# Attention in groups of three key blocks with three score slots, and a depthwise convolution taken wholly by TensorE

## The chip, the cores and the metric

The kernel runs on one core of a Trainium2 chip. The metric is device time in microseconds (us) of one launch. Before the change it is 4289.91 us, the median of three runs (4288.64 to 4290.33). Lines like `L223` are lines of the kernel before the change unless "after" is said; in the changed kernel the same statements stand some lines further on (the score product is L223 in both, the projections move from L397 and L409 to L405 and L417, the depthwise convolution from L873 to L880).

## The reference

Four residual layers over `x` of shape (4, 256, 48, 48), so B = 4 images, 256 channels, N = 2304 positions, all float32:

```python
x = x + L0(_gn(x))   # 8 heads of 64: q, k l2-normed over the head's 64 channels, softmax(10 q.k), v, w_out
x = x + L1(_gn(x))   # max pool, blur pool, four depthwise convolutions, sigmoid gate
x = x + L2(_gn(x))   # one head of 64: softmax(theta.phi / 8), g, W_w, batch norm over the images
x = x + L3(_gn(x))   # squeeze gate, depthwise 3x3, instance norm, leaky relu
```

```python
# layer 0
q = _l2norm_last(q)
k = _l2norm_last(k)
sim = jnp.einsum('bhdi,bhdj->bhij', q, k) * SCALE
attn = jax.nn.softmax(sim, axis=-1)
out = jnp.einsum('bhij,bhdj->bhid', attn, v)
...
# layer 3
y = xw * a[:, :, None, None]
y = jax.lax.conv_general_dilated(y, refine_w, window_strides=(1, 1), padding='SAME', feature_group_count=C, dimension_numbers=('NCHW', 'OIHW', 'NCHW'))
y = y + refine_b[None, :, None, None]
mu = jnp.mean(y, axis=(2, 3), keepdims=True)
var = jnp.mean(jnp.square(y - mu), axis=(2, 3), keepdims=True)
y = (y - mu) * jax.lax.rsqrt(var + EPS)
return jax.nn.leaky_relu(y, SLOPE)
```

## The kernel before

**Units, groups, steps.** The attention of layers 0 and 2 is one long stream of 108 units. A unit is one image, one pair of heads (layer 0) or two halves of the queries (layer 2), and 384 query columns. There are 16 phases of six units in layer 0 (image b, pair p) and four phases of three units in layer 2. The keys come in 18 blocks of 128 (`JB`). `scores(u, j)` (L223) multiplies one block of keys by the queries, once for each half of the partitions, into a PSUM tile `sc` of two banks, and ScalarE takes the exponential into an SBUF tile `pt` (L229). `weigh(u, j)` (L242) multiplies `pt` by the values and accumulates in the PSUM bank `av` over all 18 blocks. A float32 matmul appears as two PE records.

`attend` goes through the stream in steps of one group of `G = 2` blocks. In step t it issues, in this order: the scores of group t; the sums of the group before (`add_up`); what is due (`finish`); some ticks of the side work; `total`, where one is due; and `weigh` for the group before. The four engines PE, DVE, ACT and POOL keep exactly this written order (`manual_schedule`) until the attention ends. Each engine works through its own queue in order.

**The sums.** `add_up` sums the exponentials for the softmax. In groups 1, 3, 5 and 7 POOL adds the two tiles into `half` (one buffer, L259) and DVE adds `half` to `acc` in the next step (L255); in the other groups DVE adds the tiles itself (L252, L262). A unit takes 13 additions on DVE and 4 on POOL. `total` multiplies `acc` by ones into a bank `pj` (L267), and DVE takes the reciprocal `rinv` (L272, in `total`). `divide`, one step later, reads the sum on ScalarE for a check (L279), multiplies `av` by `rinv` on DVE (L282) and checks `rinv` on ScalarE (L284). Two steps follow in which one `out_proj` product each is made (L441) and added to x by DVE (L446, L450).

**The side work** comes as generators in lanes, merged tick by tick and spread over the steps of a phase. `project` makes q, k and v of the next pair: for each of six chunks, `normed` (DVE, L374), q and k products (L397), each copied out by DVE (L401) and squared by ScalarE in place (L402), and the v product (L409), copied by ScalarE (L414). In phases p = 1 and p = 2 of images 1 to 3, and in the first two phases of layer 2, a second lane runs layer 1 of the image before: pooling and 80 taps on DVE (L564). `project2` (L617, L628, L641) and `w_stats` (L663, read by `bn_stats` L675) belong to layer 2. Before the stream starts, `project` runs once alone for the first pair.

**PSUM.** Eight banks: two `sc` tiles of two banks, two `av` banks, two `pj` banks. Every product other than scores and values goes through `pj`: `total`, the projections, `out_proj`, `w_stats`, the small products of the group norms.

**Layer 3** is ordered by the framework's scheduler. For each image `before_conv` makes 12 products of W (L663), each scaled by ScalarE (L818) and added to x by POOL (L822), then a group norm and the gate (PE L174, L184, L831, L843, with DVE, POOL and ScalarE between), and at last the padded image on ScalarE (L854). `conv` makes five of the nine taps as matmuls with diagonal matrices (L873, 10 matmuls for each of three steps), ScalarE evacuates (L880), DVE adds the other four taps (L888), takes statistics (L893), ScalarE normalises (L902), DVE applies the leaky relu (L903), POOL adds to x (L904), and a DMA writes the result. The generator `before_conv(b + 1)` fills the steps of `conv(b, .)`.

```python
G = 2
NG = JB // G
PAIRED = (1, 3, 5, 7)
...
    ps_sc = ctx.enter_context(tc.tile_pool(name="ps_sc", bufs=2, space=bass.MemoryType.PSUM))
    ps_av = ctx.enter_context(tc.tile_pool(name="ps_av", bufs=2, space=bass.MemoryType.PSUM))
    ps_pj = ctx.enter_context(tc.tile_pool(name="ps_pj", bufs=2, space=bass.MemoryType.PSUM))
```

Of the kernel before, what the change touches and what calls it, by code (L numbers as in the profile page):

```python
# [9 lines left out]
F32 = mybir.dt.float32  # L10
AF = mybir.ActivationFunctionType
ALU = mybir.AluOpType
AX = mybir.AxisListType

P = 128
HW = 48
# [39 lines left out]
def _drain(gen):  # L56
    for _ in gen:
        pass
# [4 lines left out]

G = 2
NG = JB // G
PAIRED = (1, 3, 5, 7)
NCH = NSL
# [6 lines left out]
def usual_path(  # L74
# [7 lines left out]
    small = ctx.enter_context(tc.tile_pool(name="small", bufs=2))  # L82
    ps_sc = ctx.enter_context(tc.tile_pool(name="ps_sc", bufs=2, space=bass.MemoryType.PSUM))
    ps_av = ctx.enter_context(tc.tile_pool(name="ps_av", bufs=2, space=bass.MemoryType.PSUM))
    ps_pj = ctx.enter_context(tc.tile_pool(name="ps_pj", bufs=2, space=bass.MemoryType.PSUM))

# [121 lines left out]
    big = keep.enter_context(tc.tile_pool(name="big", bufs=2))  # L208
    wqp = main.enter_context(tc.tile_pool(name="wq", bufs=2))
    xsp = main.enter_context(tc.tile_pool(name="xs", bufs=3))  # L210
    op = main.enter_context(tc.tile_pool(name="o", bufs=2))
    ppool = main.enter_context(tc.tile_pool(name="pt", bufs=5))
    apool = main.enter_context(tc.tile_pool(name="acc", bufs=2))
# [33 lines left out]
    def add_up(u, g):  # L247

        pts = [u["pt"][j] for j in range(g * G, (g + 1) * G)]
        if g == 0:  # L250
            u["acc"] = apool.tile([P, 2, SL], F32, tag="acc", name="acc")
            nc.vector.tensor_add(u["acc"], pts[0], pts[1])  # L252
            return
        if u.get("half") is not None:
            nc.vector.tensor_add(u["acc"], u["acc"], u["half"])  # L255
            u["half"] = None
        if g in PAIRED:
            u["half"] = hpool.tile([P, 2, SL], F32, tag="half", name="half")
            nc.gpsimd.tensor_add(u["half"], pts[0], pts[1])  # L259
        else:  # L260
            for pt in pts:
                nc.vector.tensor_add(u["acc"], u["acc"], pt)  # L262

    def total(u):
        u["l"] = pj_tile()
        for h in range(2):
            nc.tensor.matmul(  # L267
                u["l"][h * D : (h + 1) * D, :SL], lhsT=ones, rhs=u["acc"][:, h, :],
                start=True, stop=True,
            )  # L270
        u["rinv"] = rpool.tile([P, SL], F32, tag="rinv", name="rinv")
        nc.vector.reciprocal(u["rinv"], u["l"][:, :SL])  # L272

    finished = {}

    def divide(u):
        i = u["i"]
        junk = rpool.tile([P, SL], F32, tag="junk", name="junk")
        nc.scalar.activation(  # L279
            junk, u["l"][:, :SL], AF.Identity, accum_out=checks[:, 0, i : i + 1]  # L280
        )
        nc.vector.tensor_mul(u["o"](), u["av"][:, :SL], u["rinv"])  # L282
        finished[u["b"]] = finished.get(u["b"], 0) + 1
        nc.scalar.activation(  # L284
            junk, u["rinv"], AF.Identity, accum_out=checks[:, 1, i : i + 1]
        )
# [18 lines left out]
    def attend(phases):  # L305
# [7 lines left out]
        def finish(t):  # L313
            for fn in due.pop(t, ()):
                fn()

        for t, (u, g, st) in enumerate(groups):
            for j in range(g * G, (g + 1) * G):
                scores(u, j)
            if prev is not None:  # L320
                add_up(*prev)
            finish(t)
            if st["gen"] is None:
# [4 lines left out]
            until = -(-st["total"] * st["at"] // (st["n"] - 3))  # L328
            while st["done"] < until and next(st["gen"], st) is not st:
                st["done"] += 1  # L330
            if st["at"] == st["n"] - 1:
                _drain(st["gen"])
            if t in sums:
                total(sums.pop(t))
            if prev is not None:
                pu, pg = prev
                for j in range(pg * G, (pg + 1) * G):
                    weigh(pu, j)
                if pg == NG - 1:
                    sums[t + 1] = pu  # L340
                    due.setdefault(t + 2, []).append(lambda pu=pu: divide(pu))
                    for i, fn in enumerate(pu["after"]):
                        due.setdefault(t + 3 + i, []).append(fn)
            prev = (u, g)
        pu, pg = prev
        add_up(pu, pg)
        for j in range(pg * G, (pg + 1) * G):
            weigh(pu, j)
        for t in sorted(due):
            finish(t)  # L350
# [9 lines left out]
    def project(b, norm, pair):  # L360
# [18 lines left out]
        fetch(0)  # L379
        fetch(1)  # L380
        q = big.tile([P, N], F32, tag="q", name="q")
# [6 lines left out]
        for s in range(NCH):  # L388
            cols = slice(s * SL, (s + 1) * SL)
            if s + 1 < NCH:  # L390
                normed(s + 1)
            if s + 2 < NCH:
                fetch(s + 2)
            for t, to in ((0, q), (1, kk)):
# [12 lines left out]
            for i in range(SL // P):  # L407
# [7 lines left out]
                v[:, j0 : j0 + SL // P, :].rearrange("p j d -> p (j d)"), ps[:, :SL]  # L415
            )
            yield  # L417
        n2 = small.tile([P, 2], F32, tag="n2", name="n2")
# [371 lines left out]


    PE_TAPS = (0, 1, 2, 3, 5)
    DVE_TAPS = (4, 6, 7, 8)
    diag = lp.tile([P, NK, len(PE_TAPS), P], F32, name="diag")
    for k in range(NK):
        for i, t in enumerate(PE_TAPS):
            nc.gpsimd.tensor_scalar(diag[:, k, i, :], ident, rfw[:, k, t : t + 1], None, ALU.mult)
    W2 = HW + 2
# [64 lines left out]
    def conv(b, k):  # L863
# [3 lines left out]
        for c in range(NSL // 2):  # L867
            ps = sc_tile()
            for h in range(2):
                r0 = (2 * c + h) * RS  # L870
                for t in PE_TAPS:
                    dr, dc = divmod(t, 3)
                    nc.tensor.matmul(  # L873
                        ps[:, h, :SL].rearrange("p (r c) -> p r c", c=HW),
                        lhsT=diag[:, k, PE_TAPS.index(t), :],
                        rhs=pad[:, r0 + dr : r0 + dr + RS, dc : dc + HW],
                        start=t == PE_TAPS[0], stop=t == PE_TAPS[-1],
                    )
# [3 lines left out]
                bias=vec[:, V_RB, k : k + 1],  # L882
            )
            yield
        zr = z.rearrange("p (r c) -> p r c", c=HW)
        for t in DVE_TAPS:
            dr, dc = divmod(t, 3)
            nc.vector.scalar_tensor_tensor(  # L888
                zr, pad[:, dr : dr + HW, dc : dc + HW], rfw[:, k, t : t + 1], zr,
                ALU.mult, ALU.add,  # L890
            )
        for s in range(NSL):
            nc.vector.bn_stats(st[:, s, :], z[:, s * SL : (s + 1) * SL])  # L893
        mv = small.tile([P, 2], F32, tag="in_mv", name="in_mv")
# [4 lines left out]
        rsqrt(ri, ve)  # L899
        mr = small.tile([P, 1], F32, tag="in_mr", name="in_mr")  # L900
        nc.vector.scalar_tensor_tensor(mr, mv[:, 0:1], -1.0, ri, ALU.mult, ALU.mult)
        nc.scalar.activation(z, z, AF.Identity, bias=mr, scale=ri)  # L902
        nc.vector.scalar_tensor_tensor(z, z, SLOPE, z, ALU.mult, ALU.max)  # L903
# [857 lines left out]
```

## Time and profile before

The profiled execution took 4289.91 us, of which its span (first to last instruction) is 4287.8 us; 2.1 us lie around it. Its time equals the median of the three runs. The mean granted TensorE clock was 0.963.

| stretch of the trace (us) | what runs | PE busy | DVE busy | PE clock |
|---|---|---|---|---|
| 20.5 to 52.5 (32.0) | the first `project`, alone | 27.95 | 12.80 | 1.00 |
| 249.9 to 449.4 (199.5) | layer 0, image 0, pair 1 | 198.64 | 115.17 | 1.00 |
| 1047.9 to 1274.7 (226.8) | layer 0, image 1, pair 1, with layer 1 beside it | 210.19 | 202.14 | 0.96 |
| 3424.4 to 3581.1 (156.7) | layer 2, image 0, with layer 1 beside it | 123.39 | 136.61 | 0.88 |
| 3865.3 to 3952.7 (87.4) | layer 2, image 3 | 87.40 | 51.35 | 1.00 |
| 3952.7 to 4288.0 (335.3) | the last `w_stats`, then layer 3 | 240.13 | 196.08 | 0.79 |

Of the 16 phases of layer 0 ten last 196.4 to 199.6 us, and the six with layer 1 beside them 226.1 to 234.9 us. Busy times are sums of what the records cover; overlapping matmuls count once. A busy PE is not a PE at its peak, since the ends of matmuls are modelled.

### The profile page before, as it was taken

The page shows a single profiled execution, that of the slowest core. Times are in us where ns is not written, and L with a number is a line of the kernel's source. Part 1 is how long each engine was busy: PE and PEld are TensorE (multiplying, and loading weights), DVE is VectorE, ACT ScalarE, POOL GpSimd, SP SyncE. Part 2 cuts the span into 40 slices and gives each one's busy share as a digit, 9 for nine tenths or more (in the row PEclk, how much of TensorE's full clock was granted, in tenths as well). Part 3 has the DMA queues.
Part 4 walks back from the last instruction along what each step waited for, and adds up shares of the span by engine and source line. Part 5 has one row for each costly group of instructions (what it writes and reads, how often), then busy time and mean ns, then how long its engine had stood idle before and what let it go on. Part 6 is the DMA issues. An engine that isn't in the chain of part 4 may idle for free.

```text
span 4287.8 us, 50150 instructions
## 1 busy us (share of the span) xinstructions
PE 3954.9 (92%) x19538; PEld 1733.6 (40%) x19538; DVE 3034.9 (71%) x3751; ACT 1875.7 (44%) x3062; POOL 1088.3 (25%) x624
## 2 busy tenths in 40 slices
PE   7999999999998899999888999998889977899784
PEld 3444444444433344444333444443334433344442
DVE  4555556556998965569989655699895589955556
ACT  3444444444544444445444445454444433234331
POOL 1222222222222322222223222223232222212352
PEclk9999999999999999999999999999999988899787
DMA  4000000000000000000000000000000000000001
GB/s 148 16 16 19 8 19 8 19 12 15 12 15 12 15 8 19 12 16 12 15 12 15 6 21 12 15 12 12 12 1 1 1 1 1 1 1 1 11 33 45
DMA packets 44326, 67.45 MB, mean 16 GB/s; under 512 B 4336, under 2 KB 42032, under 8 KB 42032
## 3 DMA queue, kind: packets, MB, share of 16 engines
q1 hardware_dynamic: 41216, 62.92, 4.7%
q8 instruction: 155, 2.54, 0.2%
q10 hardware_dynamic: 2864, 1.24, 0.1%
q14 instruction: 91, 0.75, 0.1%
HBM read 54.71 MB, written 9.44 MB: 15 GB/s over the span
## 4 chain that ended last, share of the span: by engine, by line
PE 64%; DVE 29%; issue 3%; ACT 2%; POOL 2%; DMA 0%; DVEq 0%; ACTq 0%; POOLq 0%
PE sc L223 24%; PE av L242 23%; DVE acc L262 8%; DVE l1acc L564 7%; PE pj L397 5%; PE pj L441 3%; PE pj L409 2%; DVE acc L255 2%; PE sc L873 2%; DVE rinv L272 2%; DVE z L888 2%; PE pj L267 1%; PE pj L663 1%; ACT pt L229 1%; DVE xs L374 1%
## 5 line engine op out<-in xcount | busy, mean ns | idle before, releaser
L229 ACT ACTIVATE pt<-sc 128x768 f32<-128x768 f32 x1944 | 1473.6, 808 | 1520.0 <-PE sc L223 1425.3
L259 POOL TENSOR_TENSOR half<-pt 128x768 f32<-128x768 f32 x432 | 853.8, 1976 | 2626.5 <-ACT pt L229 2313.1
L223 PE MATMUL sc<-q,k 64*128 64x384 f32 x6912 | 1363.8, 513 | 52.0 <-ACT pt L229 49.1
L242 PE MATMUL av<-pt,v 128*64 128x384 f32 x6912 | 1321.0, 502 | 0.0
L262 DVE TENSOR_TENSOR acc<-acc,pt 128x768 f32<-128x768 f32 x864 | 946.1, 1095 | 128.1 <-ACT pt L229 42.3
L223 PEld LDWEIGHTS sc<-q,k 64*128 64x128 f32 x6912 | 595.9, 187 | 809.6 <-ACT pt L229 305.1
L242 PEld LDWEIGHTS av<-pt,v 128*64 128x64 f32 x6912 | 433.2, 137 | 725.7 <-issue 713.9
L255 DVE TENSOR_TENSOR acc<-acc,half 128x768 f32<-128x768 f32 x432 | 416.5, 964 | 191.9 <-POOL half L259 191.2
L564 DVE SCALAR_TENSOR_TENSOR l1acc<-pd,grid,l1acc 128x256 f32<-128x256 f32 x640 | 347.3, 543 | 18.2
L272 DVE RECIPROCAL rinv<-pj 128x384 f32<-128x384 f32 x108 | 275.9, 2555 | 109.7 <-PE pj L267 109.6
L397 PE MATMUL pj<-xs,w 128*128 128x384 f32 x768 | 303.0, 520 | 40.2 <-issue 32.7
L402 ACT ACTIVATE pj<-pj 128x384 f32<-128x384 f32 x192 | 91.2, 475 | 403.8 <-DVE q L401 266.3
L441 PE MATMUL pj<-o,wo 128*128 128x384 f32 x384 | 175.7, 539 | 39.2 <-DVE x L450 16.5
L397 PEld LDWEIGHTS pj<-xs,w 128*128 128x128 f32 x768 | 136.3, 194 | 186.0 <-issue 101.5
L450 DVE TENSOR_TENSOR x<-pj,x 128x384 f32<-128x384 f32 x144 | 79.9, 555 | 169.9 <-PE pj L441 169.9
L223 PE MATMUL sc<-qv,kd 64*128 64x384 f32 x864 | 176.5, 527 | 19.1 <-ACT pt L229 19.1
L242 PE MATMUL av<-pt,qv 128*64 128x384 f32 x864 | 192.1, 534 | 0.0
L873 PE MATMUL sc<-pad,diag 128*128 128x384 f32 x480 | 169.1, 510 | 5.7 <-ACT pad L854 5.7
L409 PE MATMUL pj<-w,xs 128*128 128x128 f32 x1152 | 152.8, 283 | 13.7 <-DVE x L450 12.2
L409 PEld LDWEIGHTS pj<-w,xs 128*128 128x128 f32 x1152 | 139.2, 193 | 60.1 <-issue 28.9
L252 DVE TENSOR_TENSOR acc<-pt 128x768 f32<-128x768 f32 x108 | 107.1, 992 | 45.2 <-ACT pt L229 44.8
L166 DVE BATCH_NORM_STATS2 gn_st<-x 128x6 f32<-128x384 f32 x192 | 98.1, 549 | 57.4 <-POOL x L822 57.4
(139 smaller groups left out, 2229.2 us busy)
## 6 DMA issues: line engine op xcount, KB each, us to landing
xs<-in_x_dram SPq DMA_DIRECT2D x96, 384.0 KB, 3.2
x<-in_x_dram SPq DMA_DIRECT2D x8, 1152.0 KB, 8.4
out_dram<-x SPq DMA_DIRECT2D x8, 1152.0 KB, 4.2
w<-in_wqkv_dram SPq DMA_DIRECT2D x32, 192.0 KB, 3.7
wo<-in_wout_dram ACTq DMA_DIRECT2D x1, 512.0 KB, 4.1
dw<-in_dww_dram ACTq DMA_DIRECT2D x1, 132.0 KB, 5.4
wph<-in_thphi_w_dram ACTq DMA_DIRECT2D x2, 64.0 KB, 4.5
Ww<-in_W_w_dram ACTq DMA_DIRECT2D x2, 64.0 KB, 5.0
```

Of the source, the lines that this page charges most:

```text
L223: nc.tensor.matmul(ps[:, h, :SL], lhsT=u["of"]["k"][r, j * P : (j + 1) * P], rhs=u["of"]["q"][r, u["qc"]], start=True, stop=True,)
L229: nc.scalar.activation(pt, ps[:, :, :SL], AF.Exp)
L242: nc.tensor.matmul(u["av"][r, :SL], lhsT=value(u, j, h), rhs=pt[:, h, :], start=j == 0, stop=j == JB - 1,)
L255: nc.vector.tensor_add(u["acc"], u["acc"], u["half"])
L259: nc.gpsimd.tensor_add(u["half"], pts[0], pts[1])
L262: nc.vector.tensor_add(u["acc"], u["acc"], pt)
L272: nc.vector.reciprocal(u["rinv"], u["l"][:, :SL])
L397: nc.tensor.matmul(ps[:, :SL], lhsT=w[:, k, t, :], rhs=xs[s][:, k, :], start=k == 0, stop=k == NK - 1,)
L409: nc.tensor.matmul(ps[:, i * P : (i + 1) * P], lhsT=xs[s][:, k, i * P : (i + 1) * P], rhs=w[:, k, 2, :], start=k == 0, stop=k == NK - 1,)
L441: nc.tensor.matmul(ps[:, :SL], lhsT=wo[:, p, k * P : (k + 1) * P], rhs=o, start=True, stop=True)
L564: nc.vector.scalar_tensor_tensor(acc, src, w, acc, ALU.mult, ALU.add)
L873: nc.tensor.matmul(ps[:, h, :SL].rearrange("p (r c) -> p r c", c=HW), lhsT=diag[:, k, PE_TAPS.index(t), :], rhs=pad[:, r0 + dr : r0 + dr + ...
```

## The change

The attention now goes in groups of three blocks (`G = 3`, six groups to a unit). There are three `sc` tiles (six banks), one `av` bank and one `pj` bank. ScalarE copies the finished `av` into SBUF (`take`, called after the last `weigh` of a unit), and `divide` multiplies that copy. `total` now also reads the sum on ScalarE for the check. In `add_up` POOL adds the first two tiles of groups 1 to 4, and DVE the third; a unit still takes 13 additions on DVE and 4 on POOL. In a step, either the due work is done or one tick, ahead of `total` and `weigh`; further ticks come after `weigh`. The buffers of `pt` go from five to seven, of `xs` from three to two, of `w` from two to one. `normed` of the next chunk moves from the start of a chunk to its end.

In layer 3 all nine taps are matmuls (18 for each of three steps); the four taps on DVE go; statistics are taken after each step, and the normalisation moves from ScalarE (L902) to DVE.

```diff
-G = 2
+G = 3
-PAIRED = (1, 3, 5, 7)
+PAIRED = (1, 2, 3, 4)
...
-    ps_sc = ctx.enter_context(tc.tile_pool(name="ps_sc", bufs=2, space=bass.MemoryType.PSUM))
-    ps_av = ctx.enter_context(tc.tile_pool(name="ps_av", bufs=2, space=bass.MemoryType.PSUM))
-    ps_pj = ctx.enter_context(tc.tile_pool(name="ps_pj", bufs=2, space=bass.MemoryType.PSUM))
+    ps_sc = ctx.enter_context(tc.tile_pool(name="ps_sc", bufs=3, space=bass.MemoryType.PSUM))
+    ps_av = ctx.enter_context(tc.tile_pool(name="ps_av", bufs=1, space=bass.MemoryType.PSUM))
+    ps_pj = ctx.enter_context(tc.tile_pool(name="ps_pj", bufs=1, space=bass.MemoryType.PSUM))
...
-    wqp = main.enter_context(tc.tile_pool(name="wq", bufs=2))
-    xsp = main.enter_context(tc.tile_pool(name="xs", bufs=3))
+    wqp = main.enter_context(tc.tile_pool(name="wq", bufs=1))
+    xsp = main.enter_context(tc.tile_pool(name="xs", bufs=2))
-    ppool = main.enter_context(tc.tile_pool(name="pt", bufs=5))
+    ppool = main.enter_context(tc.tile_pool(name="pt", bufs=7))
...
         pts = [u["pt"][j] for j in range(g * G, (g + 1) * G)]
+        half = u.pop("half", None)
+        if g in PAIRED:
+            u["half"] = hpool.tile([P, 2, SL], F32, tag="half", name="half")
+            nc.gpsimd.tensor_add(u["half"], pts[0], pts[1])
+            pts = pts[2:]
         if g == 0:
             u["acc"] = apool.tile([P, 2, SL], F32, tag="acc", name="acc")
             nc.vector.tensor_add(u["acc"], pts[0], pts[1])
-            return
...
+            pts = pts[2:]
+        if half is not None:
+            nc.vector.tensor_add(u["acc"], u["acc"], half)
+        for pt in pts:
+            nc.vector.tensor_add(u["acc"], u["acc"], pt)
...
+    def take(u):
+        u["araw"] = rpool.tile([P, SL], F32, tag="araw", name="araw")
+        nc.scalar.copy(u["araw"], u["av"][:, :SL])
...
-        nc.vector.tensor_mul(u["o"](), u["av"][:, :SL], u["rinv"])
+        nc.vector.tensor_mul(u["o"](), u["araw"], u["rinv"])
...
-            finish(t)
...
-            while st["done"] < until and next(st["gen"], st) is not st:
+            if t in due:
+                finish(t)
+            elif st["done"] < until and next(st["gen"], st) is not st:
                 st["done"] += 1
-            if st["at"] == st["n"] - 1:
-                _drain(st["gen"])
...
                 if pg == NG - 1:
+                    take(pu)
                     sums[t + 1] = pu
...
+            while st["done"] < until and next(st["gen"], st) is not st:
+                st["done"] += 1
+            if st["at"] == st["n"] - 1:
+                _drain(st["gen"])
...
             if s + 1 < NCH:
-                normed(s + 1)
-            if s + 2 < NCH:
-                fetch(s + 2)
+                fetch(s + 1)
...
+            if s + 1 < NCH:
+                normed(s + 1)
             yield
...
-    PE_TAPS = (0, 1, 2, 3, 5)
-    DVE_TAPS = (4, 6, 7, 8)
-    diag = lp.tile([P, NK, len(PE_TAPS), P], F32, name="diag")
+    diag = lp.tile([P, NK, 9, P], F32, name="diag")
...
-                for t in PE_TAPS:
+                for t in range(9):
...
-        for t in DVE_TAPS:
-            dr, dc = divmod(t, 3)
-            nc.vector.scalar_tensor_tensor(
-                zr, pad[:, dr : dr + HW, dc : dc + HW], rfw[:, k, t : t + 1], zr,
-                ALU.mult, ALU.add,
-            )
...
-        nc.scalar.activation(z, z, AF.Identity, bias=mr, scale=ri)
+        nc.vector.tensor_scalar(z, z, mv[:, 0:1], ri, ALU.subtract, ALU.mult)
```

## The prediction

> **What bounds the kernel now.** I read the page first, for where the bound changes; then the stages, by windows cut where a phase's first exponential starts; then the order of time inside one stage of each kind.
>
> ```profile
> span 4287.8 us, 50150 instructions
> ...
> PE   7999999999998899999888999998889977899784
> ...
> DVE  4555556556998965569989655699895589955556
> ...
> PEclk9999999999999999999999999999999988899787
> ...
> PE 64%; DVE 29%; issue 3%; ACT 2%; POOL 2%; DMA 0%; DVEq 0%; ACTq 0%; POOLq 0%
> ...
> L262 DVE TENSOR_TENSOR acc<-acc,pt 128x768 f32<-128x768 f32 x864 | 946.1, 1095 | 128.1 <-ACT pt L229 42.3
> ```
>
> ```profile
> 249.90:449.40 199.50, 198.64 (x1034) 85.58 (x1032) 115.17 (x131) 98.00 (x163) 44.56 (x25) 1.00 0.05 15
> 1047.90:1274.70 226.80, 210.19 (x1046) 88.64 (x1044) 202.14 (x256) 102.64 (x177) 61.69 (x33) 0.96 0.05 13
> 3952.70:4288.00 335.30, 240.13 (x666) 128.04 (x662) 196.08 (x240) 91.49 (x97) 133.81 (x91) 0.79 0.07 29
> ```
>
> The windows give span, then PE, PEld, DVE, ACT, POOL busy, and the clock. There are three regimes. Ten layer-0 phases are bound by PE (198.64 of 199.5). The six with layer 1 beside them are bound by DVE, closely followed by PE. Layer 3 is bound by neither: its chain passes from PE to DVE and back. So a gain on PE counts only in the first kind, and work moved to PE in layer 3 shows in full once PE fills it.
>
> In order of time, a PE-bound stretch, the end of the attention, and layer 3:
>
> ```profile
> 292.56 1.51 PE L242 MATMUL av<-pt,v 128*64 128x384 f32 x8
> 294.00 1.56 PE L223 MATMUL sc<-q,k 64*128 64x384 f32 x8
> 295.50 0.91 PE L441 MATMUL pj<-o,wo 128*128 128x384 f32 x2
> ...
> 3951.64 2.80 PE L242 MATMUL av<-pt,qv 128*64 128x384 f32 x16
> ...
> 3958.89 13.67 PE L663 MATMUL pj<-y,Ww 64*128 64x384 f32 x22 [2.44 <-ACT junk L279]
> ...
> 4011.72 6.72 PE L873 MATMUL sc<-pad,diag 128*128 128x384 f32 x20
> ...
> 4018.37 1.55 PE L663 MATMUL pj<-y,Ww 64*128 64x384 f32 x4
> ```
>
> Start to start, a value group takes 1.44 us and a score group 1.49; two value groups in a row end 1.29 later than one. So the passage between the two kinds costs 0.15 or more. The convolution takes 6.65 us for 20 records, 0.665 a matmul. And the projections' evacuation:
>
> ```profile
> 296.25 1.45 PE L397 MATMUL pj<-xs,w 128*128 128x384 f32 x4
> ...
> 297.74 0.56 DVE L401 COPY k<-pj 128x384 f32<-128x384 f32 x1 [0.73 <-PE pj L397]
> ...
> 298.33 0.47 ACT L402 ACTIVATE pj<-pj 128x384 f32<-128x384 f32 x1 [1.84 <-DVE k L401]
> 298.71 0.19 ACT L402 ACTIVATION_READ_ACCUMULATOR pj<-pj 128x1 f32 x1
> ```
>
> PE issues its next product at 297.63; the bank is free only at 298.90.
>
> **What the Trainium skill says.** "TensorEngine Tiling (Array Packing)", Key Properties: changing the tiling mode, not just the tile, drains TensorE. The trace agrees: pairs of score matmuls inside a group follow at 0.32, while the first and last of a group take 0.42 to 0.43. "PSUM — Partial Sum Buffer", PSUM bank collisions: two engines on one bank and quadrant must be kept apart by semaphores, so one bank for all products means one product at a time until the last reader is done. The trace agrees: PE waits 2.44 us for the check L279 above. "SBUF — State Buffer", two separate sides: a DVE instruction with two SBUF inputs and a GpSimd one exclude each other for a whole instruction. Here L262 takes 959 ns in the PE-bound phase and 1353 where POOL gets in between. "TensorE: Matmul & The Clock Gate", Part 1: an idle PE falls to half clock. Here one W product takes 1.28 us at the end of the attention and 0.74 between convolutions.
>
> **The change part by part.** The sum is made against the profiled execution's 4289.9 us (span 4287.8 and 2.1 around it), which is the median as well.
>
> *Groups of three, where PE binds.* A pair of matmuls adds 0.32 to a group, so three blocks take (1.49 + 0.64) + (1.44 + 0.64) = 4.21 us, against 1.5 x 2.93 = 4.395: 0.185 less, six times a unit, 1.11 a unit. In the 60 units of the ten phases: -66.6.
>
> *One bank, where PE binds.* In the built order of the changed kernel `total` (L267) comes straight after a q or k product twice, and after a v product once, in each of six phases (pairs 0 to 2 of image 0, pair 0 of the others); once each in pair 3 of images 0 to 2; four `project2` products in the last. After q or k PE stalls 298.96 - 297.63 = 1.33; after v 0.65 (ScalarE copy 0.48 and hand-overs), and the same after a `project2` product. That is 6 x 3.3 + 3 x 2.0 + 2.6 = +28. Elsewhere at least 2.1 us of scores or values lie between two products and cover the 1.33; if DVE is late there, the cover is gone. Sum of both: -38.
>
> *Work hidden here.* `take` (0.48 on ScalarE, 44% busy) ends under the next scores before `av` is needed. The third score slot and seven `pt` keep the old slack of one tile. The check now stands right behind `total` on ScalarE and waits for the reciprocal (2.56), with the next exponentials queued behind it; three free slots let PE go on through all three scores. With one `w` buffer its load starts when the last v product is done, steps before use.
>
> *Where DVE binds, layer 0.* DVE has the same 13 additions; POOL's `half` still waits for DVE's addition of the previous one and then blocks a DVE instruction (about 1.4 us, 24 times a phase). What changes is idle time: DVE now idles 15 to 17 us a phase, 5 to 7 of them near the start, where PE waits for `normed` behind DVE's queue. The earlier `normed` takes part of that. Bounds: all idle and nothing more gone, -95; twice the present loss from the one bank, +60. I take -25 for the six.
>
> *Layer 2.* Images 2 and 3 gain 6 x 1.11 = 6.7 and pay about ten adjacent products at 0.7. Images 0 and 1 are near DVE's bound; fifteen adjacent products, most beside DVE work: +3. In all +3, between -15 and +20.
>
> *Start.* The first `project` has nothing to cover it. Warm chunk with two banks: 32 us / 6 = 5.3. With one: q and k each 1.49 (start to DVE) + 0.04 + 0.56 + 0.03 + 0.66 + 0.06 = 2.85, v 1.79 + 0.48 + 0.06 = 2.3: 8.0, +16. If the gaps keep the clock low, each product takes 1.3 to 1.4 longer: 12.2, +41. I take +26. The `xs` load of the next chunk (3.2 to landing) hides under a chunk.
>
> *W products ahead of layer 3.* 24 of them, at the low clock. Now they follow at 1.28. With one bank: 1.68 from start to DVE (3958.89 to 3960.57) + 0.57 + 0.06 = 2.3 for twelve with `bn_stats`, +13; 1.74 + 0.67 + 0.06 = 2.47 for twelve with ScalarE, +14. The first padding no longer stands behind a W evacuation: -2. Sum +25.
>
> *Nine taps.* An image has 108 diagonal matmuls instead of 60: 108 x 0.665 = 71.8. The built order sets ten W products between them, at 0.8: 8. Two matmuls (1.33) between two of these cover ScalarE's 0.67. The second group-norm product L184 stands behind the whole of the second half's convolution, so the chain to the next padded image stays bare: L184 to convolution is 3993.87 to 4002.35 now, 8.5; the cold restart then costs 2 (8.60 for the first 20 records against 6.65). Sum 71.8 + 8 + 0.4 + 8.6 + 2.3 = 91.1 an image, against 4071.51 - 4002.35 = 69.2 now: +21.9, three times: +66. Removed with it, per half: four L888 (2.6 to 3.2) and L902 on ScalarE (2.3); added on DVE one pass (L425 has the shape: 1.42). All that lies beside 36 us of PE and counts only in the tail. Last image: 71.8 + 2.3, then 0.9 evacuation, 1.1 statistics, 0.5, power 0.75, 1.45, 2.6, POOL 5.1, and 5.6 from POOL's end to the span's end: 18. Together 92.3, against 4287.8 - 4209.87 = 77.9: +14. Layer 3 with its W products: 25 + 66 + 14 = +105, between 90 and 120.
>
> *Sum.* 26 - 38 - 25 + 3 + 105 = +71: 4289.9 + 71 = 4361 us.
>
> **The rivals.**
> (a) Faster. The mixed phases lose their idle time and much of POOL's interference: a larger group smooths DVE's bursts. For it: the six last 226 to 235 us, while PE alone needs about 193. Against: DVE is busy 202 to 209 of that with unchanged work. It decides from the point where each of the six shortens by 16 instead of 4. At 24 each (-144) and -20 in layer 2: 4361 - 119 - 23 = 4219.
> (b) Slower still. In the mixed phases the one bank ties PE to a late DVE, and DVE then starves behind `total`: the product, the square on ScalarE and L267 make 1.9 us of DVE idle, and more in layer 2. For it: PE already waits there for `out_proj` and W banks. Against: DVE's additions use the previous step's tiles, which are there. At +10 a phase (+60) and +15: 4361 + 85 + 12 = 4458.
> (c) Layer 3 costs half. The group-norm chain slips under the convolution, so an image takes 82: 4361 - 27 = 4334. Against: the built order.
> (d) The switch saving isn't there, because it is PE's own start-up per group whatever its size: the 66.6 falls away, 4428. Against: 1.29 for the second value group.
>
> **How the numbers follow.** Forecast 0.62, (a) 0.12, (b) 0.12, (c) 0.08, (d) 0.06. The forecast's own range is 4361 with the mixed phases -60 to +30 about my value, start -8 to +15, layer 3 -15 to +15: about 4300 to 4420. To leave no more than 2 in 10 outside I reach toward both sides: 4290 to 4430. A difference under 0.2% (9 us) can't be told from none. Faster than that: 0.12 from (a), less its mild half, plus the low end of the forecast: 0.11. Same: 0.06. Slower: 0.83.
>
> **What would show it.** Right: layer-0 phases without layer 1 at 195 to 197 us; convolution matmuls 0.33 a record with an image every 91 us; W products 2.3 us apart before layer 3; the first scores near 78 us. Wrong: mixed phases under 212 us or over 236; convolution restarts without the 8 us gap; stalls of PE ahead of L267 of more than 1.5 us, which would mean that DVE comes late even where PE binds.

## The result, and the profile after

The changed kernel takes 4419.61 us (median; 4415.05 to 4423.38) against 4289.84 us before. The ratio is 1.030, with a 95% interval of 1.0285 to 1.032: it is slower, by 130 us. The time forecast was 4361 us. The profiled execution took 4415.05 us, with a span of 4413.3 us.

First the page of the changed kernel, the rows that answer to those shown of before:

```profile
span 4413.3 us, 51038 instructions
...
PE   6999999999888999998889999988899867997997
...
DVE  3565566556888856578887555788865788562222
...
PEclk9999999999999999999999999999999878996999
...
PE 69%; DVE 25%; ACT 2%; issue 2%; POOL 2%; DMA 0%; DVEq 0%; ACTq 0%; POOLq 0%
...
L262 DVE TENSOR_TENSOR acc<-acc,pt 128x768 f32<-128x768 f32 x864 | 886.9, 1027 | 97.8 <-ACT pt L229 23.8
```

The last digits of DVE's row fall from 5 to 2: in layer 3 VectorE is busy for about a quarter of the time now, and PE for most of it. In the chain that ended last PE's share rises from 64 to 69%; the page's list of the chain's lines has the convolution at 7% (L880), where it was 2% (L873).

Then the same three stages, by windows (columns as before):

```profile
263.50:459.90 196.40, 193.25 (x1034) 88.42 (x1032) 115.55 (x131) 97.70 (x169) 55.45 (x25) 1.00 0.05 15
1049.90:1276.60 226.70, 201.45 (x1040) 92.27 (x1038) 190.63 (x255) 102.59 (x182) 66.66 (x32) 0.96 0.05 13
3977.00:4413.30 436.30, 378.96 (x1058) 196.64 (x1054) 112.49 (x208) 74.81 (x90) 111.31 (x99) 0.87 0.05 22
```

The first is the phase of 199.5 us, now 196.4, with 3.15 us of PE idle where there were 0.86. The second is the surprise: PE needs 8.7 us less (201.45 for 210.19) and DVE 11.5 us less (190.63 for 202.14), and yet the phase lasts as long as before. Both engines only wait longer; VectorE is idle for 36.1 us instead of 24.7. The third is layer 3 with the last W products.

All stages, each measured from first exponential to first exponential (layer 2 to the end of the last exponential; in layer 3 from first convolution to first convolution, the last image to the end of the span), in us of the profiled executions. "Mixed" phases below are those with layer 1 beside them:

| stage | before | after | change | forecast |
|---|---|---|---|---|
| start, to the first exponential | 53.5 | 70.9 | +17.4 | +26 |
| ten phases bound by PE | 1990.0 | 1961.9 | -28.1 | -38 |
| six phases with layer 1 beside them | 1381.0 | 1391.3 | +10.3 | -25 |
| layer 2 | 528.3 | 552.8 | +24.5 | +3 |
| W products, to the first convolution | 49.7 | 75.4 | +25.7 | +25 |
| four images of layer 3 | 285.4 | 360.9 | +75.5 | +80 |

Layer 3, the phases bound by PE and the start came out near the working. The missing 55 us are in the mixed phases and in layer 2. Two kinds of hold stand behind most of them; a hold is the time for which a product's bank is taken, from the product to the end of its last reader.

**In the mixed phases it is `total`.** PE's waits in the whole changed kernel (engine and line, what it waited for, us in total, times, longest):

```profile
PE pj L267 <- ACT pj L410: 58.5, 32, 4.7
PE pj L417 <- ACT junk L275: 49.6, 12, 8.1
PE sc L223 <- ACT pt L229: 34.7, 17, 12.0
...
PE pj L405 <- ACT junk L275: 24.4, 6, 6.0
```

The first row is a `total` that waits until ScalarE has squared a q or k product in the bank. The forecast counted this stall where PE binds (18 of the 58.5 us); the other 40 lie in the mixed phases. The rows with L275 are products that wait until `total`'s own readers, the reciprocal and the check, are through. With the smaller rows of this kind they make about 95 us, 76 of them in the mixed phases, and the forecast had no term for them. Here is the longest, a timeline of one mixed phase, PE first, then DVE:

```profile
1443.62 0.87 PE L267 MATMUL pj<-acc,ones 128*64 128x384 f32 x4 [0.36 <-DVE acc L262]
1444.32 2.10 PE L242 MATMUL av<-pt,v 128*64 128x384 f32 x12
1454.51 2.93 PE L417 MATMUL pj<-w,xs 128*128 128x128 f32 x12 [8.09 <-ACT junk L275]
1457.37 3.62 PE L223 MATMUL sc<-q,k 64*128 64x384 f32 x12
```

```profile
1443.48 4.53 DVE L574 SCALAR_TENSOR_TENSOR l1acc<-pd,grid,l1acc 128x256 f32<-128x256 f32 x6
1447.92 0.95 DVE L257 TENSOR_TENSOR acc<-pt 128x768 f32<-128x768 f32 x1
1448.98 0.96 DVE L262 TENSOR_TENSOR acc<-acc,pt 128x768 f32<-128x768 f32 x1
1449.86 1.52 DVE L574 SCALAR_TENSOR_TENSOR l1acc<-pd,grid,l1acc 128x256 f32<-128x256 f32 x3
1451.29 2.55 DVE L272 RECIPROCAL rinv<-pj 128x384 f32<-128x384 f32 x1
```

The sum is in the bank at 1444.5. VectorE still has seven of these layer-1 taps and two additions to do before it comes to the reciprocal, and the check L275 follows at 1453.88. Until then no other product may start, and the v product stands for 8.09 us, with the next scores behind it. The idle PE then restarts slowly: the v product takes 2.93 us (1.60 in a PE-bound phase), the scores 3.62 (2.21). Over all 108 units the bank stays taken after `total` for 3.22 us at least (reciprocal and check), in the mixed phases for 3.2 to 10.0, in all for 479 us.

The late products come back to VectorE. Its waits for q and k products over two mixed phases, now (1049.9 to 1513.4) and before (1047.9 to 1506.7):

```profile
DVE q L409 <- PE pj L405: 13.5, 7, 4.6
DVE k L409 <- PE pj L405: 10.6, 6, 3.6
```

```profile
DVE q L401 <- PE pj L397: 2.5, 2, 1.9
DVE k L401 <- PE pj L397: 0.7, 1, 0.7
```

So PE waits for a bank that a late VectorE holds, and VectorE then waits for the product that PE could not start.

**In layer 2 it is rather layer 2's own products.** Image 1 loses most of all its stages, 20 us; first in the changed kernel, then before (windows):

```profile
3580.90:3769.20 188.30, 136.91 (x594) 64.32 (x592) 153.48 (x222) 50.67 (x84) 47.12 (x23) 0.83 0.00 1
```

```profile
3581.10:3749.50 168.40, 135.63 (x590) 61.31 (x588) 154.74 (x220) 50.19 (x81) 39.64 (x21) 0.85 0.00 1
```

The work is the same to within 1.3 us on PE and DVE; the stage is 20 us longer. So it is waiting, but hardly for `total`. PE's waits inside this stage (the three largest for the product bank, and the first of those for the check):

```profile
PE pj L673 <- DVE qv L655: 9.4, 3, 7.4
PE pj L267 <- DVE kd L631: 7.8, 2, 4.7
PE pj L651 <- DVE bst L685: 6.2, 2, 3.5
PE pj L638 <- ACT junk L275: 1.3, 1, 1.3
```

Here the bank is held by VectorE's own copies and statistics of layer 2's products (L631, L642, L655, L685): about 40 us of PE's waits, where the same readers made 11 before, against 2 for the check.

### The profile page after: what moved, and what is told of

Same layout as the page of the kernel before. It is cut to its first block, busy times and chain, and to the rows that moved or that the text cites. A ratio compares the mean times of both kernels' runs of the same rounds, so it can differ in the third digit from the quotient of the medians.

```text
span 4413.3 us, 51038 instructions
## 1 busy us (share of the span) xinstructions
PE 4010.0 (91%) x19922; PEld 1868.3 (42%) x19922; DVE 2889.6 (65%) x3719; ACT 1856.7 (42%) x3162; POOL 1228.9 (28%) x632
## 4 chain that ended last, share of the span: by engine, by line
PE 69%; DVE 25%; ACT 2%; issue 2%; POOL 2%; DMA 0%; DVEq 0%; ACTq 0%; POOLq 0%
PE sc L223 23%; PE av L242 22%; DVE l1acc L574 7%; PE sc L880 7%; PE pj L405 6%; DVE acc L262 5%; PE pj L451 3%; PE pj L417 3%; DVE acc L260 2%; DVE rinv L272 2%; PE pj L673 2%; PE pj L267 2%; POOL half L253 1%; DVE acc L257 1%; PE pj L651 1%
## 5 line engine op out<-in xcount | busy, mean ns | idle before, releaser
L229 ACT ACTIVATE pt<-sc 128x768 f32<-128x768 f32 x1944 | 1438.0, 811 | 806.5 <-PE sc L223 742.8
L253 POOL TENSOR_TENSOR half<-pt 128x768 f32<-128x768 f32 x432 | 1019.2, 2359 | 2419.0 <-DVE acc L260 1401.3
L223 PE MATMUL sc<-q,k 64*128 64x384 f32 x6912 | 1289.3, 506 | 17.6 <-ACT pt L229 16.1
L242 PE MATMUL av<-pt,v 128*64 128x384 f32 x6912 | 1249.7, 496 | 0.0
L262 DVE TENSOR_TENSOR acc<-acc,pt 128x768 f32<-128x768 f32 x864 | 886.9, 1027 | 97.8 <-ACT pt L229 23.8
L880 PE MATMUL sc<-pad,diag 128*128 128x384 f32 x864 | 298.3, 502 | 5.2 <-ACT pad L861 5.2
L275 ACT ACTIVATE junk<-pj 128x384 f32<-128x384 f32 x108 | 53.0, 491 | 431.9 <-DVE rinv L272 431.9
L880 PEld LDWEIGHTS sc<-pad,diag 128*128 128x128 f32 x864 | 164.9, 194 | 135.7 <-issue 29.0
L409 DVE COPY q<-pj 128x384 f32<-128x384 f32 x96 | 53.4, 557 | 209.2 <-PE pj L405 209.2
L267 PE MATMUL pj<-acc,ones 128*64 128x384 f32 x432 | 99.0, 538 | 89.7 <-ACT pj L410 58.5
```

The source lines that it names most:

```text
L223: nc.tensor.matmul(ps[:, h, :SL], lhsT=u["of"]["k"][r, j * P : (j + 1) * P], rhs=u["of"]["q"][r, u["qc"]], start=True, stop=True,)
L229: nc.scalar.activation(pt, ps[:, :, :SL], AF.Exp)
L242: nc.tensor.matmul(u["av"][r, :SL], lhsT=value(u, j, h), rhs=pt[:, h, :], start=j == 0, stop=j == JB - 1,)
L880: nc.tensor.matmul(ps[:, h, :SL].rearrange("p (r c) -> p r c", c=HW), lhsT=diag[:, k, t, :], rhs=pad[:, r0 + dr : r0 + dr + RS, dc : dc + HW],
```

## The experiments

Twelve kernels, each timed in three rounds beside the kernel before. The stage columns are of one profiled execution each, in us, cut as above.

| run | median | ratio, 95% interval | start | 10 PE-bound | 6 mixed | layer 2 | W | images |
|---|---|---|---|---|---|---|---|---|
| before | 4289.84 | | 53.5 | 1990.0 | 1381.0 | 528.3 | 49.7 | 285.4 |
| after | 4419.61 | 1.0285 to 1.032 | 70.9 | 1961.9 | 1391.3 | 552.8 | 75.4 | 360.9 |
| a1_layer3_back | 4354.01 | 1.0129 to 1.0163 | 73.6 | 1963.6 | 1388.9 | 560.0 | 74.6 | 293.8 |
| a2_taps_alone | 4354.48 | 1.0132 to 1.0166 | 53.0 | 1988.7 | 1383.4 | 528.3 | 49.7 | 348.8 |
| a4_total_short | 4360.77 | 1.0146 to 1.018 | 76.4 | 1961.5 | 1347.9 | 540.7 | 74.3 | 360.7 |
| a6_layer2_scalar | 4404.78 | 1.0252 to 1.0287 | 71.0 | 1961.0 | 1391.3 | 542.2 | 74.9 | 359.4 |
| b1_qk_short | 4398.62 | 1.0239 to 1.0273 | 63.6 | 1952.8 | 1384.2 | 554.5 | 74.9 | 359.8 |
| b2_order_back | 4465.97 | 1.0391 to 1.0426 | 72.7 | 2001.4 | 1400.9 | 562.0 | 74.3 | 358.5 |
| b3_groups_of_two | 4619.9 | 1.0747 to 1.0783 | 76.8 | 2013.8 | 1521.3 | 574.8 | 74.1 | 360.5 |
| b4_all_short | 4221.07 | 0.9821 to 0.9854 | 54.4 | 1953.0 | 1348.0 | 528.2 | 51.9 | 287.1 |
| c1_check_first | 4420.11 | 1.0289 to 1.0323 | 72.7 | 1964.0 | 1392.1 | 553.5 | 74.5 | 361.4 |
| c2_spare_bank | 4363.26 | 1.0156 to 1.019 | 53.8 | 1962.5 | 1391.8 | 552.9 | 50.1 | 348.8 |
| c3_two_slots | 4607.71 | 1.0723 to 1.0759 | 54.2 | 2153.2 | 1447.4 | 551.4 | 50.5 | 349.2 |
| c4_whole_change_repaired | 4280.74 | 0.9969 to 0.9986 | 53.2 | 1952.4 | 1345.3 | 525.8 | 51.9 | 348.4 |

A stage that a run doesn't touch repeats within a few us, layer 2 within about 7 (552.8 to 560.0) and the start within about 6 (70.9 to 76.8; the last section says why), so smaller differences are not read.

**The two halves apart.** The changed kernel with layer 3 as before (taps, statistics and normalisation):

```diff
-                for t in range(9):
+                for t in PE_TAPS:
...
+        for t in DVE_TAPS:
...
-        nc.vector.tensor_scalar(z, z, mv[:, 0:1], ri, ALU.subtract, ALU.mult)
+        nc.scalar.activation(z, z, AF.Identity, bias=mr, scale=ri)
```

> The changed kernel with layer 3 as before (five taps on TensorE, four on VectorE, ScalarE normalises); attention and banks as changed. If the loss adds up stage by stage, the last exponential ends at 3977 as in the changed kernel, the W products ahead of the first convolution still take 75 us instead of 50, and an image takes 69 us as before: profile span about 4313 + 26 = 4338, time about 4340. Rival: the one bank of products also binds inside layer 3 when the convolution is short (few matmuls between W products), then an image takes 75 or more and the time is 4360 or more.

And the kernel before with the reverse of that edit:

> The kernel before with only layer 3 changed (nine taps on TensorE, VectorE normalises), two product banks. If the taps cost by themselves what the changed trace shows, images take about 91 us, the last one 90, and the time is 4290 + 75 = 4365. Rival (the group-norm chain slips under the convolution once the product bank is free earlier): images take 84 or less, time 4340 or less.

The first took 4354, not 4340. Images take 73.4, 71.4, 70.8 and 78.3 us where they took 69.2, 68.7, 69.7 and 77.9, so the one bank does bind inside layer 3, by 8.4 us together; less than the rival's. The rest of the miss lies in layer 2 (+7.2) and the start (+2.7), which this edit doesn't touch. The taps alone took 4354, not 4365: images of 86 us, not 91 and not 84. Nine taps cost 63 us on two banks, and the single bank adds 12 to that (360.9 against 348.8). So each half is slower than before by itself: the attention half is not faster at all.

**The bank behind `total`.** ScalarE reads the sum first and leaves a copy, and the reciprocal works on the copy:

```diff
-        nc.vector.reciprocal(u["rinv"], u["l"][:, :SL])
...
         nc.scalar.activation(
             junk, u["l"][:, :SL], AF.Identity, accum_out=checks[:, 0, i : i + 1]
         )
+        nc.vector.reciprocal(u["rinv"], junk)
```

> The changed kernel, but ScalarE reads the sum at once and writes it to SBUF, and the reciprocal reads that copy; so the bank and ScalarE's queue no longer wait for the reciprocal (2.56 us, and whatever VectorE has queued ahead of it). Theory: the 94 us in which TensorE waits for the check, and the exponentials queued behind it, are a good part of the loss in the stages with layer 1 and in layer 2: about 3 less in each of the six mixed phases, 15 less in layer 2, nothing in the phases bound by TensorE; time about 4385. Rival: those stages are bound by VectorE's work alone and the waits lie beside it; time 4415 to 4420.

It gave 59 us, more than the 35 expected: 43 in the mixed phases and 12 in layer 2, none where PE binds. In layer 2 the 12 come from images 0 and 2; image 1, which loses most, only goes from 188.3 to 187.5, and PE's waits there stay those for layer 2's own products. The bank is now taken for 0.64 us (median) after `total`, 105 us in all instead of 479. That run freed two things at once, the bank and ScalarE's queue, in which the exponentials stood behind the check. So a second edit freed the queue alone, by exchanging the two statements while both still read the bank:

```diff
-        nc.vector.reciprocal(u["rinv"], u["l"][:, :SL])
...
         nc.scalar.activation(
             junk, u["l"][:, :SL], AF.Identity, accum_out=checks[:, 0, i : i + 1]
         )
+        nc.vector.reciprocal(u["rinv"], u["l"][:, :SL])
```

> The changed kernel with two statements of the total exchanged: ScalarE reads the sum before VectorE takes the reciprocal; both still read the bank, so the bank is held until the reciprocal ends, but ScalarE's queue no longer waits for it. If it is the exponentials queued behind the check that made the 59 us of the run with the short total, this gives most of it: 4360 to 4380. If it is the bank held through the reciprocal, 4405 to 4420.

It gave nothing. ScalarE's waits, in the changed kernel and then in this run, show that the queue was freed:

```profile
ACT junk L275 <- DVE rinv L272: 431.9, 108, 10.1
```

```profile
ACT junk L274 <- PE pj L267: 65.8, 42, 7.5
```

Its check (L274 there) now waits 65.8 us in all, for the product only. PE's waits in the same run show that the bank was not:

```profile
PE pj L417 <- DVE rinv L277: 44.8, 6, 7.5
PE pj L405 <- DVE rinv L277: 28.9, 6, 5.3
```

Together they are as long as those on the check were, and have another name. It is the bank, held through a late reciprocal; the queue on ScalarE was harmless, as the forecast had said of it.

**The bank behind q and k.** ScalarE squares the copy in SBUF instead of the bank:

```diff
+                sq = rpool.tile([P, SL], F32, tag="sq", name="sq")
                 nc.scalar.activation(
-                    ps[:, :SL], ps[:, :SL], AF.Square, accum_out=ss[:, t, s : s + 1]
+                    sq, to[:, cols], AF.Square, accum_out=ss[:, t, s : s + 1]
                 )
```

> The changed kernel, but ScalarE squares the copies of q and k in SBUF instead of the bank, so the bank is free after VectorE's copy. If the stalls are what the prediction made of them (bank held 1.33 us past TensorE's next product, 0.7 of it by ScalarE), each stall behind a q or k product falls to about 0.65: twelve of them in the six chunks of the start give -8, ten phases bound by TensorE -8, the mixed phases a few: time about 4400. Rival: ScalarE isn't what holds the bank, and nothing changes: 4415 or more.

As expected: 4399, the start 7.3 shorter, the PE-bound phases 9.1, the mixed ones 7.1. The stalls behind q and k fall from 1.32 to 0.65 us.

**Layer 2's evacuations.**

```diff
-            nc.vector.tensor_scalar(kd[:, cols], ps[:, :SL], thphib[:, 1:2], None, ALU.add)
+            nc.scalar.activation(
+                kd[:, cols], ps[:, :SL], AF.Identity, bias=thphib[:, 1:2], scale=1.0
+            )
...
-                nc.vector.bn_stats(bst[:, k, b * NSL + s, :], ps[:, :SL])
+                wsb = rpool.tile([P, SL], F32, tag="wsb", name="wsb")
+                nc.scalar.copy(wsb, ps[:, :SL])
+                nc.vector.bn_stats(bst[:, k, b * NSL + s, :], wsb)
```

> The changed kernel, but in layer 2 ScalarE instead of VectorE evacuates the k product and copies the W products before their statistics, so the bank isn't held behind VectorE's queue. Theory (in layer 2 the one bank ties TensorE to a late VectorE, which then starves): layer 2 takes about 530 instead of 553 us, time about 4397. Rival: layer 2 is bound by what VectorE has to do, which hardly changes (12 fewer passes of 0.5 us per image at most): 4413 or more.

Layer 2 took 542: half of what was expected. Image 1 alone went from 188.3 to 181.4. With all holds short (below) it is 176, still 8 above before. With two product banks, two score slots and no hold shortened (`c3_two_slots`, below) it is 174.9, so the rest does not hang on the single bank alone; what makes it is open.

**The spare bank.** Before and after the attention nobody uses the value bank, so products take the two in turn there:

```diff
+        spare["n"] += 1
+        if spare["on"] and spare["n"] % 2:
+            return ps_av.tile([P, 512], F32, tag="av", name="av")
         return ps_pj.tile([P, 512], F32, tag="pj", name="pj")
...
+    spare["on"] = False
     attend(phases)
+    spare["on"] = True
     _drain(w_stats(B - 1))
```

> The changed kernel with the value bank lent to the products in turn with the product bank, before the attention and after it; nothing changes inside the attention. If the single bank alone made the losses there, the first exponential comes 17 to 18 earlier, the stretch to the first convolution is 50 instead of 75, and images take 86 instead of 88 to 92: 4420 - 18 - 25 - 12 = 4365. Rival (the low clock, or the late group norm, makes part of it): 4385 or more.

4363 for 4365, with all three terms: the first exponential at 53.8, W products 50.1, images 86.4, 87.5, 84.8 and 90.1. The start, the W products and 12 us of layer 3 are the single bank and nothing else.

**Groups, slots and order.** Three parts of the attention half, each undone alone. Groups of two:

```diff
-G = 3
+G = 2
...
-PAIRED = (1, 2, 3, 4)
+PAIRED = (1, 3, 5, 7)
```

> The changed kernel with groups of two blocks again (banks, slots, order and buffers as changed). Theory (each passage between scores and values costs TensorE): in the phases bound by TensorE scores and values take 7.3 us more a phase, over ten phases +73; beside layer 1 less; time 4470 to 4500. Rival (the passage costs nothing of its own, the rate follows the matmuls): 4410 to 4430.

4620, far over both. In the PE-bound phases the groups of three are worth 52 us, less than the 73 of the theory. In the mixed phases they are worth 130, which neither theory had. So the one bank with groups of two loses 140 us there against before (1521 against 1381), groups of three win 130 back, and the small +10 of the table is the difference of two large terms. Which share of the 140 is the bank's and which the new order's, with its one tick per step, was not separated.

The banks of before, two of each:

```diff
-    ps_sc = ctx.enter_context(tc.tile_pool(name="ps_sc", bufs=3, space=bass.MemoryType.PSUM))
-    ps_av = ctx.enter_context(tc.tile_pool(name="ps_av", bufs=1, space=bass.MemoryType.PSUM))
-    ps_pj = ctx.enter_context(tc.tile_pool(name="ps_pj", bufs=1, space=bass.MemoryType.PSUM))
+    ps_sc = ctx.enter_context(tc.tile_pool(name="ps_sc", bufs=2, space=bass.MemoryType.PSUM))
+    ps_av = ctx.enter_context(tc.tile_pool(name="ps_av", bufs=2, space=bass.MemoryType.PSUM))
+    ps_pj = ctx.enter_context(tc.tile_pool(name="ps_pj", bufs=2, space=bass.MemoryType.PSUM))
```

> The changed kernel with the banks of before: two score slots, two value banks, two product banks. The third score product of a group then waits until the first exponential is through (0.81 us and hand-overs, against 0.70 us of one more score product): about 0.45 us a step, 648 steps, +250 or somewhat less; the second product bank gives back 110: 4500 to 4570. Rival (the third slot isn't needed, the one product bank made the loss): 4310 to 4350.

Slower still, 4608. PE's waits of that run:

```profile
PE sc L223 <- ACT pt L229: 373.4, 645, 14.2
```

Almost each of the 648 steps waits for an exponential, 0.58 us on average, so the estimate of 0.45 was low. Groups of three need the third slot, and with eight banks the third slot leaves one bank each for values and products. The change has no better split of the banks; what it can choose is how long each is held.

The order of before:

```diff
-            if t in due:
-                finish(t)
-            elif st["done"] < until and next(st["gen"], st) is not st:
+            finish(t)
+            while st["done"] < until and next(st["gen"], st) is not st:
                 st["done"] += 1
+            if st["at"] == st["n"] - 1:
+                _drain(st["gen"])
```

with the ticks after `weigh` taken out.

> The changed kernel with the side work issued in the order of before (what is due and all ticks ahead of the total and the values). Theory (the banks cost, the order only spreads the products): more products stand next to one another on one bank, so the phases bound by TensorE get longer by 5 to 10 each and the time is 4460 to 4520. Rival (the new order, with side work after the values, is what delays VectorE beside layer 1): the mixed phases and layer 2 fall back to 226 to 235 and 528, time 4390 or less.

4466: 40 us more where PE binds, 10 more in the mixed phases; the 9 in layer 2 are little above what that stage varies by. The new order is part of what makes one bank bearable.

**All holds short.** The edits of a4, a6, b1 and c2 together, first with layer 3 as before, then with the changed one:

> The changed attention with every hold of the product bank shortened (sum read by ScalarE at once, q and k squared in SBUF, layer 2's k and W products evacuated by ScalarE), the idle value bank lent to the products before and after the attention, and layer 3 as before. If the losses are those of the bank and of layer 3, the first exponential is at 55, the ten phases bound by TensorE at 193 to 195, the six mixed ones at 220 to 228, layer 2 at 520, the W products and layer 3 at 335 as before: 55 + 1940 + 1345 + 525 + 335 = 4200 to 4225. If they aren't, it stays over 4270.

> The run with all holds shortened and the spare bank lent (4221), but with the changed layer 3 (nine taps). If the taps cost on two banks what they cost alone (63 more than before's layer 3), 4221 + 63 = 4284, no different from before. Rival (the shorter holds let the group norm under the convolution): 4250 or less.

4221 and 4281, as expected. The first beats both kernels: 69 us less than before (ratio 0.9837, interval 0.9821 to 0.9854). The second, the whole change with its bank mended, is at 0.9977 of before. The three medians split the result, taken in this order: groups of three, three slots and the new order with short holds, 4221.07 - 4289.84 = -69; nine taps, 4280.74 - 4221.07 = +60; the long holds of the single bank, with no spare bank lent, 4419.61 - 4280.74 = +139. The sum is +130. The single repairs do not simply add: in the mixed phases a4 alone gives 1347.9 and all holds short 1348.0, so b1's 7 us there are not on top of a4's 43.

## Why the prediction was right or wrong

The side, slower, was right, and the range held the time; the loss was 130 us where 71 were forecast, and the time lies between the forecast and rival (b), nearer to (b). It was layer 3 with its W products that made the side right (+101 where +105 was forecast). The attention with its start was forecast to gain 34 us (26 - 38 - 25 + 3) and lost 24. Signs of being wrong that the prediction had named came true as well: three mixed phases lasted 236.6 to 236.9 us, and PE stood up to 4.7 us ahead of L267.

*Start, +26, was +17.4.* The single bank cost about the 16 that were worked out, with stalls of 1.32, 1.32 and 0.57 us a chunk. Of the further 10, for products that run slowly between the gaps, little was there in this execution: only its first product took 2.93 us, the others 1.56 to 1.60. In the executions of a4 and b3, which have the same start, five products took 2.93 us and the start was longer by 22.9 and 23.3 us. So the term was real, and its size is different from execution to execution.

*Where PE binds, -38, was -28.1.* The mechanism was right on both sides. In order of time:

```profile
264.64 2.16 PE L242 MATMUL av<-pt,v 128*64 128x384 f32 x12
266.73 2.21 PE L223 MATMUL sc<-q,k 64*128 64x384 f32 x12
268.87 1.56 PE L405 MATMUL pj<-xs,w 128*128 128x384 f32 x4
271.69 0.87 PE L267 MATMUL pj<-acc,ones 128*64 128x384 f32 x4 [1.26 <-ACT pj L410]
```

Start to start, a value and a score group take 2.09 + 2.14 = 4.23 us, where 4.21 was forecast; all score and value groups of this phase fall from about 158 us to 151.7, waits apart, 6.3 less where 6.7 was forecast. The stalls are 1.26, 1.32 and 0.57 (forecast 1.33, 1.33, 0.65). Short were small things that the sum had left out: stalls apart, a q or k product takes 1.50 us from start to start instead of 1.47, a `v` product 1.54 instead of 1.50 and an `out_proj` 0.84 instead of 0.81, together about 1 us a phase. Rival (d), that there is no saving, fell.

*Mixed phases, -25, was +10.3; layer 2, +3, was +24.5.* This is the step that failed: "Elsewhere at least 2.1 us of scores or values lie between two products and cover the 1.33; if DVE is late there, the cover is gone." The sentence names the case and then prices it at nothing. It took the longest hold of the bank to be the one behind a q or k product. The longest is behind `total`: reciprocal and check hold it for 3.22 us with VectorE at once at hand, and up to 10 with layer 1's taps queued ahead. Only the check's place in ScalarE's queue was looked at, and that place was worth nothing (c1). Made short, this hold returned 43 us in the mixed phases (a4), where the miss was 35. In layer 2, where the miss was 21.5 and the bound of +20 was passed as well, it returned only 12, and nearly nothing in image 1: there the failed term is the hold of layer 2's own products by a late VectorE. The forecast had counted "fifteen adjacent products, most beside DVE work", and put them at +3. Moving two of these readers to ScalarE (a6) returned about 11 in layer 2, 7 of them in image 1. The upper bound for the mixed phases held, but its price was guessed from the present loss, not from a hold times the number of products behind it.

*The gain in the mixed phases.* -25 was set as a part of VectorE's idle time (the 15 to 17 us named there are its longer waits only; the window shown has 24.7 us of idle in 226.8). It can be read as two terms, -130 and +140 (b3), of which the forecast saw neither size. Rival (a) had the gain's side right, that larger groups help most beside layer 1; rival (b) had the place of the loss and its loop, one bank that ties PE to a late VectorE, which then starves. The hold that (b) priced, the product and its square, was the smaller part: short q and k holds returned 7 us there, a short `total` 43.

*W products +25, layer 3 +80: +25.7 and +75.5.* An image takes 92.1, 90.3, 88.2 and 90.3 us where 91.1 and 92.3 for the last were worked out. PE in the first image, in order of time:

```profile
4105.15 19.62 PE L880 MATMUL sc<-pad,diag 128*128 128x384 f32 x60
4124.61 0.28 PE L174 MATMUL pj<-gn_mv,gmat 128*128 128x2 f32 x2
4124.75 11.86 PE L880 MATMUL sc<-pad,diag 128*128 128x384 f32 x36
4136.44 0.28 PE L184 MATMUL pj<-gn_sq,gmat 128*128 128x2 f32 x2
4138.02 0.39 PE L838 MATMUL pj<-pm,w 128*64 128x1 f32 x4 [1.30 <-DVE pm L835]
```

L184 does stand behind the whole convolution, and the next one starts at 4144.46, 8.0 us later (forecast 8.5): rival (c), that the chain slips under the convolution, did not happen here. With two banks an image took 86 us (a2), but not in that way: the next convolution still began 7.0 us after the last (4082.31 to 4089.33), and it was the stretch of the convolution itself that was shorter (79 us for 84). The removed VectorE and ScalarE work shows no gain, as forecast: PE waits for only 12.5 us in all four images. No run takes that work away alone.

*What the Trainium skill had said.* "PSUM — Partial Sum Buffer", PSUM bank collisions, counts two reads of one bank by two engines as a collision too. The trace agrees as far as it goes: in the changed kernel no check starts before its reciprocal has ended, 108 times of 108; no run here lets the two overlap. The forecast used the page for "one product at a time until the last reader is done", and then did not follow `total` to its last reader.

## What to carry to other kernels

When several uses are put on one buffer, list every use with the time from its producer's start to its last reader's end, queues of the readers included, and compare the longest of them (not the one next to the edit) with the work that lies before the next producer. If a reader sits on an engine that is often late, let an idle engine copy the data out first: here exchanging two statements and one operand returned 59 us, and shortening all the holds turned a 3% loss into a change that is about level with before. A stage that a forecast moves by a little may hold two large terms of opposite sign, and only an experiment that undoes one part alone shows them.

## What was not expected of the hardware

Neither the share of busy time nor the gaps decide alone how fast PE runs. Two windows of the changed kernel, the start and the W products ahead of layer 3 (the clock is the third number from the end):

```profile
21.90:67.40 45.50, 26.83 (x109) 15.05 (x108) 10.95 (x24) 9.38 (x29) 0.00 (x0) 1.00 0.46 174
3984.00:4012.40 28.40, 19.84 (x26) 6.00 (x26) 9.24 (x19) 0.53 (x2) 8.32 (x25) 0.50 0.00 0
```

At the start PE is busy for 59% of the time, with gaps of up to 1.33 us, and its products take 1.56 us. In the W products it is busy for 70%, with gaps of 0.66 us, and stays at half. That it takes such gaps to hold it there is ruled out by the kernel before, where PE does W products without a gap for 10.5 us and stays at half as well:

```profile
3962.00:3972.50 10.50, 10.50 (x19) 4.25 (x18) 5.61 (x10) 0.00 (x0) 0.57 (x8) 0.50 0.00 0
```

The start is not fixed either. The same product with the same stall ahead of it, in the changed kernel and in a4, whose edit doesn't touch the start:

```profile
24.55 1.56 PE L405 MATMUL pj<-xs,w 128*128 128x384 f32 x4 [1.26 <-ACT pj L410]
```

```profile
24.64 2.93 PE L405 MATMUL pj<-xs,w 128*128 128x384 f32 x4 [1.26 <-ACT pj L410]
```

In a4 the first five products take 2.93 us, up to 39.6 us, and the sixth 1.60; the clock column reads 1.00 for that stretch in both runs, so it is the products' own durations that show the slow state. What decides it, the history, the form of the matmuls (128 rows against 64) or something else, no run here tells apart.
